# Attention, then a selective scan, on one core: results asked for later, the gate's phase in smaller steps, B and C in the pool of delta u

## The chip, the core and the metric

The kernel runs on one core of one Trainium2 chip. The metric is the device time of one execution in microseconds; the median of several executions counts. Profiles are of one execution each. The engines have short names: PE (TensorE, matmuls; PEld its weight loads), DVE (VectorE), ACT (ScalarE), POOL (GpSimd) and SP (SyncE, which issues the DMAs; SPq is its queue). "L994" is line 994 of the kernel.

## What is computed

There are 16 images of 256 channels by 1024 positions, in f32. Each goes through two layers, and every layer adds to its input what it makes of the group norm of it:

```python
x = x + attention_block(group_norm(x))   # layer norm, 4 heads of 32, softmax, out projection,
                                         # layer norm, feed forward with gelu, residuals
x = x + scan_block(group_norm(x))
# scan_block, L = 1024, 512 inner channels, 64 states:
ctx = sigmoid(conv3(x) + gate_b)
u, z = split(x @ in_proj.T)
u = silu(causal_conv4(u) + conv_b)
dt, B, C = split(u @ x_proj.T)
delta = softplus(dt @ dt_proj.T + dt_b)
h[t] = exp(delta[t] * A) * h[t-1] + (delta[t] * u[t]) * B[t]     # 512 x 64 states, over t
y[t] = sum over states of h[t] * C[t]
out = ((y + u * D) * silu(z)) @ out_proj.T * ctx
```

## The kernel before

**The scan, in units.** The states of one image are 256 tiles of 128 rows by 1024 positions: two channels times 64 states each. One tile is a *unit*. For a unit, SP loads `delta u` of its two channels, spread over the 64 states, into a tile `dub` of the pool `dutp` (`load`, L972); POOL multiplies it by B (`inputs`, L977); PE forms delta in all rows (`decay`, L986) and ACT its exponential in PSUM (L988); DVE scans along the positions (`scan`, L994). Loads run 6 units ahead, products 4, decays 2. The PSUM pool of the decays has two tiles, so PE can begin the decay for unit n + 2 only when the scan of unit n has ended. Eight units fill one tile `h`, and while the next eight are scanned, `outputs` (L1011) reduces it over the states with small matmuls against C: 16 pieces `(r, s)` of 16 matmul records each, two pieces at each step, then copies and a store. There are two tiles `h`, used in turn, so the scan that begins a tile waits until PE has read its old content. B and C lie spread over 128 rows in the tiles `bt` and `ct` of the pool `hst`, one buffer each, loaded when the first unit of an image is loaded (L958 to L963). `ct` is read early in the image (`spread_c`, L1000), `bt` by every product.

**Beside the scan.** While image b is scanned, the other work runs in between: the norm, attention and scan inputs of image b + 1 (`first_norm`, `attention_layer`, `scan_inputs`), and the gate, output projection and store of image b - 1 (`gate_and_store`). Each is a generator that issues some instructions and then yields a *share*. The loop at the end (L1073 to L1114) issues, for each unit, the load, the product, a step of `outputs`, the scan, the decay and then as many steps of the side work as are due. A share under 1 is waited for as it is; a larger one is divided by a rate, but is at least one unit. `rate_for` chooses the rate so that the side work fills 247 of the image's 256 units; it is fed by the shares that the first `prepare(0)` yielded and by the list `GATE` (L859), which stands for the gate's. At unit 250 what is left is issued at once, and the next image but one is loaded.

**Order.** The instructions of PE, ACT, DVE and POOL are held in the order in which they are issued in the program (L1125 to L1135). So an instruction on DVE that follows a matmul in the same step stands behind the unit's scan, and PE does that matmul behind the unit's decay. `psum` takes a bank from the two of pool `mm`, `psum3` from these and the one of `accp` in turn; outside the scan both take free banks from a larger set.

**The places that the change touches.** `group_norm` (L272): sums over a group by PE in two steps, then the reduction on DVE (`mean_of`, L282); twice, for mean and variance. `first_norm` (L369) takes the first loads of the gate along (`besides`). In `attention_layer`: the difference of the two halves of the keys, `kd` (L448); `evacuate` (L521), which copies a head's values (`ao`) and its softmax sums from PSUM (L523, L524), once right behind the last value matmuls and once a step later; the reciprocal of the sums, which goes through DRAM three times (L567 to L586, `den`, `few`); `ao` times the reciprocal (L591), the out projection (L600) and its addition (L596, L605); the residual add of the image (L615), the feed forward (L618, L625, L635, L631). In `scan_inputs` the step before the first tap of the convolution (L749). In the gate's phase: `gate_loads` (L861), the four steps that form `(y + D u) * z` (L883 on DVE, L887 on POOL), the projection `project` (L905, four matmuls of two records each), `join` with the context (L916), the turn back into channel order (`turn_back`, L918) and its addition to the residual (`finish`, L900).

Of the kernel before, what the change touches and what calls it, by code (L numbers as in the profile page):

```python
# [3 lines left out]

# [15 lines left out]
P = 128  # L20
C = 256
KC = C // P
L = 1024
# [27 lines left out]
def attention_then_scan_kernel(  # L51
# [30 lines left out]
    dutp = pool("dutp", 7)  # L82
# [189 lines left out]
    def group_norm(src, dst):  # L272
# [18 lines left out]
        yield 1  # L291
# [15 lines left out]
        yield 1  # L307
# [61 lines left out]
    def first_norm(b, besides=()):  # L369
# [9 lines left out]
        yield from along(group_norm(xs, gn), fetches(tok, pos) + [None] * 3 + list(besides))  # L379
# [5 lines left out]
    def attention_layer(b):  # L385
# [41 lines left out]
        for i in range(2):  # L427
            for hf in range(2):
# [5 lines left out]
                if i == 1:  # L434
                    nc.scalar.copy(k4[:, hs(hf)], ps)
# [12 lines left out]
        nc.vector.tensor_tensor(kd, k4[:, hs(0)], k4[:, hs(1)], ALU.subtract)  # L448
# [118 lines left out]
        den = dram.tile([2, HEADS, L], F32, name="den", tag="den")  # L567
        nc.sync.dma_start(den[0], sums[::DH, :])
        few = small.tile([P, HEADS * L // P], F32, name="few", tag="few")
        rows = [den[i].rearrange("h (p c) -> (h p) c", c=HEADS * L // P) for i in range(2)]  # L570
        yield 1
        nc.sync.dma_start(few, rows[0])
        yield 1
        tok = []
        for go in fetches(tok, kept):
            go()
            yield 0.5
        yield 0.5
        nc.vector.reciprocal(few, few)
        yield 1  # L580
        nc.sync.dma_start(rows[1], few)
        yield 1
        for h in range(HEADS):
            nc.sync.dma_start(sums[ts(h, DH)], den[1, h : h + 1].partition_broadcast(DH))
            if h % 2 == 1:
                yield 0.5  # L586
        yield 0.5
        yield 0.5
        outs = []
        for hf in range(2):  # L590
            nc.vector.tensor_tensor(ao[:, hs(hf)], ao[:, hs(hf)], sums[:, hs(hf)], ALU.mult)  # L591
            for k in range(KC):
                for i, ps in outs:
                    if i == k:
                        t = tok[k][:, hs(0)]
                        nc.vector.scalar_tensor_tensor(t, ps, col("b_out", k), t, ALU.add, ALU.add)  # L596
            outs.clear()
            for k in range(KC):
                ps = psum("o_ps")
                nc.tensor.matmul(ps, wout_s[:, 0, ts(k, P)], ao[:, hs(hf)], start=True, stop=True)  # L600
                outs.append((k, ps))
            yield 1.3
        for k, ps in outs:
            t = tok[k][:, hs(1)]
            nc.vector.scalar_tensor_tensor(t, ps, col("b_out", k), t, ALU.add, ALU.add)  # L605
        del outs, ps
        yield 1.2
# [19 lines left out]
        outs = []  # L627
        for hf in range(3):
            for k, ps in enumerate(outs):
                t = xs[k][:, hs(hf - 1)]  # L630
                nc.vector.scalar_tensor_tensor(t, ps, col("b_ff2", k), t, ALU.add, ALU.add)  # L631
            outs = []
            for k in range(KC if hf < 2 else 0):
                ps = psum("f2_ps")
                nc.tensor.matmul(ps, wff2_s[:, 0, ts(k, P)], hdn[:, hs(hf)], start=True, stop=True)  # L635
                outs.append(ps)
            yield 1.2
# [3 lines left out]
    def scan_inputs(b):  # L641
# [107 lines left out]
        yield 1  # L749
# [109 lines left out]
    GATE = ([0.6, 0.6, 0.4] * ND)[:-1] + [1.3] * 8 + [1]  # L859

    def gate_loads(b):  # L861
# [11 lines left out]
        st["gate"] = ys, us, zs, gs, xs, wo_s, come[4:]  # L873
        return come[:4]

    def gate_and_store(b):
# [20 lines left out]
        def finish():  # L897
            for o, hf, ps in turned:
# [4 lines left out]
            turned.clear()  # L903

        def project(o, k):  # L905
            ps = psum3("m_ps")
            for d in range(ND):
                nc.tensor.matmul(  # L908
                    ps, wo_s[:, d, ts(k, P)], us[d][:, hs(o)],
                    start=(d == 0), stop=(d == ND - 1),  # L910
                )
            return ps

        def join(o, k, ps):
            v = gated[o, k] = hwork("v")
            nc.vector.scalar_tensor_tensor(v, gs[k][:, hs(o)], 1.0, ps, ALU.add, ALU.mult)  # L916
# [11 lines left out]
        work_on = [("p", 0, 0), ("p", 0, 1), ("p", 1, 0), ("t", 0, 0), ("p", 1, 1), ("t", 0, 1), ("t", 1, 0), ("t", 1, 1)]  # L928
        joined = []
        for what, o, i in work_on:  # L930
            for j in joined:
                join(*j)
            joined.clear()
            finish()
            if what == "p":
                joined.append((o, i, project(o, i)))
            else:
                turn_back(o, i)
            if come:
                come.pop(0)()  # L940
            yield 1.3
        finish()
# [248 lines left out]
```

## Time and profile before

| | us |
|---|---|
| times of three runs | 12563.84, 12565.47, 12583.97 |
| median | 12565.47 |
| the profiled execution | 12592.85 |
| its span, first to last instruction | 12590.8 |
| first scan starts | 413.69 |
| first scans of images 6 and 7 (from 0) | 4991.59, 5757.93 |
| granted clock of PE, mean | 0.82 |

The costliest groups of instructions: the columns are line, engine, operation, tiles out and in, count, busy us and mean ns of one, then the idle time of the engine before them and what ended most of it.

```profile
L977 POOL TENSOR_TENSOR dub<-dub,bt 128x1024 f32<-128x1024 f32 x4096 | 9752.7, 2404 | 2130.0 <-DMA dub<-dus 1928.2
L994 DVE TENSOR_TENSOR_SCAN h<-a,dub 128x1024 f32<-128x1024 f32 x4096 | 9166.7, 2273 | 596.0 <-ACT a L988 314.3
L988 ACT ACTIVATE a<-a,acol 128x1024 f32<-128x1024 f32 x4096 | 4466.1, 1090 | 3125.6 <-PE a L986 3065.8
```

The scan and the product for it take most of DVE and POOL. An idle time of an engine costs only where that engine is what the rest waits for.

### The profile page before, as it was taken

The page shows a single profiled execution, that of the slowest core. Times are in us where ns is not written, and L with a number is a line of the kernel's source. Part 1 is how long each engine was busy: PE and PEld are TensorE (multiplying, and loading weights), DVE is VectorE, ACT ScalarE, POOL GpSimd, SP SyncE. Part 2 cuts the span into 40 slices and gives each one's busy share as a digit, 9 for nine tenths or more (in the row PEclk, how much of TensorE's full clock was granted, in tenths as well). Part 3 has the DMA queues.
Part 4 walks back from the last instruction along what each step waited for, and adds up shares of the span by engine and source line. Part 5 has one row for each costly group of instructions (what it writes and reads, how often), then busy time and mean ns, then how long its engine had stood idle before and what let it go on. Part 6 is the DMA issues. An engine that isn't in the chain of part 4 may idle for free.

```text
span 12590.8 us, 419601 instructions
## 1 busy us (share of the span) xinstructions
PE 9574.8 (76%) x183984; PEld 5140.4 (41%) x183984; DVE 11064.3 (88%) x7355; ACT 7506.0 (60%) x10792; POOL 10050.9 (80%) x4233
## 2 busy tenths in 40 slices
PE   6686877868778687886868778687786877868777
PEld 2343434434344343443434344343443434434344
DVE  2788998989989899898989989899898998989998
ACT  3565665656656565665656656566565655656554
POOL 0587878878788787887878878787887878878798
PEclk8887988879788797987879888797887978879756
DMA  1566666676766766666676666766666666676666
GB/s 53 189 229 238 224 221 234 228 243 215 232 235 226 240 225 228 232 226 234 227 238 219 225 233 225 243 218 226 231 227 236 219 225 236 224 239 225 229 238 225
DMA packets 1070400, 2819.80 MB, mean 224 GB/s; under 512 B 324433, under 2 KB 402513, under 8 KB 1068562
## 3 DMA queue, kind: packets, MB, share of 16 engines
q1 hardware_dynamic: 1068562, 2792.97, 65.3%
q8 instruction: 1437, 23.54, 0.8%
q14 instruction: 401, 3.28, 0.1%
HBM read 2513.82 MB, written 261.62 MB: 220 GB/s over the span
## 4 chain that ended last, share of the span: by engine, by line
DVE 37%; PE 31%; issue 13%; ACT 8%; DMA 7%; POOL 3%; SPq 1%; DVEq 0%; POOLq 0%; ACTq 0%
DVE h L994 28%; PE a L986 5%; PE yb L1019 5%; ACT a L988 4%; DMA dub<-dus 3%; POOL dub L977 3%; PE av L535 2%; DVE over L453 2%; PE st_ps L547 2%; PE m_ps L908 2%; PE z_ps L684 2%; PE s_ps L473 2%; DMA xs<-ud 2%; DVE u L720 1%; PE gn_v_ps L275 1%
## 5 line engine op out<-in xcount | busy, mean ns | idle before, releaser
L977 POOL TENSOR_TENSOR dub<-dub,bt 128x1024 f32<-128x1024 f32 x4096 | 9752.7, 2404 | 2130.0 <-DMA dub<-dus 1928.2
L994 DVE TENSOR_TENSOR_SCAN h<-a,dub 128x1024 f32<-128x1024 f32 x4096 | 9166.7, 2273 | 596.0 <-ACT a L988 314.3
L988 ACT ACTIVATE a<-a,acol 128x1024 f32<-128x1024 f32 x4096 | 4466.1, 1090 | 3125.6 <-PE a L986 3065.8
L986 PE MATMUL a<-pieces,pick 48*128 48x512 bf16 x8192 | 1875.8, 448 | 2444.5 <-DVE h L994 2333.4
L1019 PEld LDWEIGHTS yb<-h,cd 128*32 128x32 f32 x131072 | 2433.3, 126 | 2822.9 <-issue 1601.6
L1019 PE MATMUL yb<-h,cd 128*32 128x64 f32 x131072 | 3189.4, 248 | 341.0 <-ACT y L1025 203.3
L986 PEld LDWEIGHTS <-pick 48*128 48x128 bf16 x8192 | 594.4, 95 | 2852.7 <-issue 2194.0
L1025 ACT COPY y<-yb 128x256 f32<-128x256 f32 x2048 | 766.5, 374 | 699.1 <-PE yb L1019 691.4
L1031 PE MATMUL yb<-turn,y 128*32 128x16 f32 x32768 | 590.7, 214 | 5.3 <-issue 4.4
L555 ACT ACTIVATE pt<-st_ps 128x512 f32<-128x512 f32 x1024 | 554.3, 599 | 63.8 <-PE st_ps L547 62.6
L535 PE MATMUL av<-pt,vv 128*64 128x512 f32 x2048 | 588.9, 655 | 3.8 <-ACT sums L524 1.6
L547 PE MATMUL st_ps<-sp 33*128 33x512 f32 x2048 | 573.6, 626 | 3.3 <-ACT pt L555 3.3
L1031 PEld LDWEIGHTS yb<-turn,y 128*32 128x32 f32 x32768 | 572.4, 159 | 6.0 <-issue 4.5
L1035 ACT COPY yo<-yb 128x128 f32<-128x128 f32 x512 | 136.4, 266 | 488.9 <-PE yb L1031 472.3
L734 PE MATMUL g_ps<-xp,w 128*128 128x512 f32 x732 | 406.9, 668 | 0.0
L473 PE MATMUL s_ps<-kd,qm 64*128 64x512 f32 x1022 | 340.6, 612 | 21.2 <-DVE kd L448 14.6
L453 DVE CUSTOM_DVE_ANT_0 over<-s_ps,over 128x512 f32<-128x512 f32 x512 | 325.9, 671 | 24.7 <-PE s_ps L473 24.4
L720 DVE SCALAR_TENSOR_TENSOR u<-up,cwh,u 128x1024 f32<-128x1024 f32 x192 | 295.8, 1541 | 28.0 <-ACT u L712 27.7
L481 ACT ACTIVATE over<-s_ps 128x512 f32<-128x512 f32 x511 | 275.2, 594 | 41.4 <-PE s_ps L473 41.4
L908 PE MATMUL m_ps<-xs,w 128*128 128x512 f32 x504 | 279.2, 704 | 10.2 <-POOL xs L887 9.4
L706 PE MATMUL u_ps<-xp,w 128*128 128x512 f32 x512 | 280.0, 674 | 1.5 <-ACT u L712 1.4
L661 POOL TENSOR_TENSOR xp<-xp,xs 128x1024 f32<-128x1024 f32 x32 | 75.1, 2349 | 254.1 <-DVE xp L313 246.5
(183 smaller groups left out, 7316.7 us busy)
## 6 DMA issues: line engine op xcount, KB each, us to landing
dub<-dus SPq DMA_DIRECT2D x4096, 512.0 KB
dps<-pc SPq DMA_DIRECT2D x384, 128.0 KB
pieces<-dps SPq DMA_DIRECT2D x1024, 48.0 KB
xs<-in_x_dram SPq DMA_DIRECT2D x64, 512.0 KB
xs<-kept SPq DMA_DIRECT2D x64, 512.0 KB
zs<-z SPq DMA_DIRECT2D x64, 512.0 KB
ud<-u SPq DMA_DIRECT2D x64, 512.0 KB
dus<-du SPq DMA_DIRECT2D x64, 512.0 KB
```

The costliest lines, as they stand in the source:

```text
L453: nc.vector.tensor_tensor_reduce(r, s, r, 1.0, -3.0e38, ALU.add, ALU.max, mx[:, at : at + 1])
L473: nc.tensor.matmul(s, qm[c // NJ][r, c % NJ], keys[r], start=True, stop=True)
L535: nc.tensor.matmul(av[ts(e, 2 * DH)], vv[j // (NJ // 2)][:, j % (NJ // 2), 2 * pair + e, :], pts[e], start=(j == 0), stop=(j == NJ - 1),)
L547: nc.tensor.matmul(s, ka[r, ts(j, P)], qa[r, hs(hf)], start=True, stop=True)
L555: nc.scalar.activation(pt, s, AF.Exp)
L977: nc.gpsimd.tensor_tensor(v, v, blocks[units[n][0]]["bt"], ALU.mult)
L986: nc.tensor.matmul(a[:, hs(hf)], w, pieces[r], start=True, stop=True)
L988: nc.scalar.activation(a, a, AF.Exp, scale=acol[:, at : at + 1])
L994: nc.vector.tensor_tensor_scan(now["h", e][:, i, :], decays.pop(n), loaded.pop(n), 0.0, ALU.mult, ALU.add)
L1019: nc.tensor.matmul(yb[ts(g, 32), ts(s, 64)], cd[:, at // 16, ts(c, 32)], hbuf[:, :, at : at + 8], start=(c == 0), stop=(c == 1),)
L1025: nc.scalar.copy(y2[:, r], yb[:, :256])
L1031: nc.tensor.matmul(some[ts(r, 32), x], y2[:, r, x:256:8], turn[:, x], start=True, stop=True)
```

## The change

- `group_norm`: the share behind the second pair of sums is 2, not 1, so the reduction comes later; likewise behind the second projection before the first tap.
- `first_norm`: six loads of the gate go along with the norm in place of four, and begin one step earlier.
- Keys: `kd` reads the second half of the keys from PSUM; a step of its own follows.
- Softmax sums: the copy out of PSUM is DVE's, not ACT's. The reciprocal no longer goes through DRAM: small matmuls bring the sums onto 128 rows, DVE takes the reciprocal from PSUM, ACT spreads it, PE turns it back, and `ao` is multiplied by it out of PSUM. The out projection and the second feed forward matmul share one routine with one bank per step; the residual add L615 is POOL's.
- Gate: the projections are issued in halves by a written plan with 15 steps in place of 8, each result used a step or more later; `GATE` grows accordingly.
- `outputs`: the last step but one takes three pieces, the last one.
- `bt` and `ct` are taken from `dutp`, which has 9 tiles, not 7.
- In the last image the side work begins at unit 12, not 8.

```diff
-    dutp = pool("dutp", 7)
+    dutp = pool("dutp", 9)
...
         sum_of(src[1], s, 1)
-        yield 1
+        yield 2
...
         del qs, q
-        yield 1
+        yield 2
...
-        yield from along(group_norm(xs, gn), fetches(tok, pos) + [None] * 3 + list(besides))
+        yield from along(group_norm(xs, gn), fetches(tok, pos) + [None] * (2 if besides else 8) + list(besides))
...
                     nc.scalar.copy(k4[:, hs(hf)], ps)
+                    keys = ps
...
-        nc.vector.tensor_tensor(kd, k4[:, hs(0)], k4[:, hs(1)], ALU.subtract)
+        nc.vector.tensor_tensor(kd, k4[:, hs(0)], keys, ALU.subtract)
+        yield 1
...
-            nc.scalar.copy(sums[ts(h, DH), hs(hf)], av[o + DH : o + 2 * DH])
+            nc.vector.tensor_copy(sums[ts(h, DH), hs(hf)], av[o + DH : o + 2 * DH])
...
-        den = dram.tile([2, HEADS, L], F32, name="den", tag="den")
-        nc.sync.dma_start(den[0], sums[::DH, :])
...
-            nc.sync.dma_start(sums[ts(h, DH)], den[1, h : h + 1].partition_broadcast(DH))
...
+        for j in range(NJ):
+            nc.tensor.matmul(ps[:, j], sums[:, ts(j, P)], ident[:, ::DH], start=True, stop=True)
+        fetch(tok, kept, 0)
+        yield 2
+        nc.vector.reciprocal(few, ps)
+        wide_few = work("wide_few").rearrange("p (j h d) -> p j h d", j=NJ, h=HEADS)
+        nc.scalar.copy(wide_few, few.unsqueeze(3).to_broadcast([P, NJ, HEADS, DH]))
+        wide_few = wide_few.rearrange("p j h d -> p j (h d)")
+        fetch(tok, kept, 1)
+        yield 2
+        inv = []
+        for hf in range(2):
+            ps = psum3("inv_ps")
+            for j in range(NJ // 2):
+                w = wide_few[:, hf * (NJ // 2) + j]
+                nc.tensor.matmul(ps[:, ts(j, P)], w, ident, start=True, stop=True)
+            inv.append(ps)
+            yield 1
+
+        def times(hf):
+            nc.vector.tensor_tensor(ao[:, hs(hf)], ao[:, hs(hf)], inv[hf], ALU.mult)
...
+        def outputs_of(w, x, to, bias, ahead=None):
+            a, c = output(w, x, 0, 0), output(w, x, 0, 1)
+            if ahead:
+                ahead()
+            yield 1.4
+            add_to(to, a, bias, 0, 0)
+            add_to(to, c, bias, 0, 1)
+            a = output(w, x, 1, 0)
+            yield 1
+            add_to(to, a, bias, 1, 0)
+            c = output(w, x, 1, 1)
+            yield 1
+            add_to(to, c, bias, 1, 1)
+            yield 1
...
+        yield from outputs_of(wout_s, ao, tok, "b_out", partial(times, 1))
...
-            nc.vector.tensor_tensor(xs[hf], xs[hf], tok[hf], ALU.add)
-            ps = psum("f1_ps")
+            nc.gpsimd.tensor_tensor(xs[hf], xs[hf], tok[hf], ALU.add)
+            ps = psum3("f1_ps")
...
+        yield from outputs_of(wff2_s, hdn, xs, "b_ff2")
...
         project(0, 1)
-        yield 1
+        yield 2
...
-    GATE = ([0.6, 0.6, 0.4] * ND)[:-1] + [1.3] * 8 + [1]
+    GATE = ([0.6, 0.6, 0.4] * ND)[:-1] + [1.3] * 9 + [1] * 6
...
-        st["gate"] = ys, us, zs, gs, xs, wo_s, come[4:]
-        return come[:4]
+        st["gate"] = ys, us, zs, gs, xs, wo_s, come[6:]
+        return come[:6]
...
+        def project(o, k, part):
+            if part == 0:
+                banks[o, k] = psum3("m_ps")
+            for d in (2 * part, 2 * part + 1):
                 nc.tensor.matmul(
-                    ps, wo_s[:, d, ts(k, P)], us[d][:, hs(o)],
+                    banks[o, k], wo_s[:, d, ts(k, P)], us[d][:, hs(o)],
                     start=(d == 0), stop=(d == ND - 1),
                 )
...
-        work_on = [("p", 0, 0), ("p", 0, 1), ("p", 1, 0), ("t", 0, 0), ("p", 1, 1), ("t", 0, 1), ("t", 1, 0), ("t", 1, 1)]
...
+        plan = "p000 p001 p010 p011j00 p100 p101j01 t00 p110j10 p111f t01 j11 t10f t11 f f"
+        for what in plan.split():
...
-            yield 1.3
-        finish()
+            yield 1.3 if "p" in what else 1
...
-            bt = hst.tile([P, L], F32, name="bt", tag="bt")
-            ct = hst.tile([P, L], F32, name="ct", tag="ct")
+            bt = dutp.tile([P, L], F32, name="bt", tag="dub")
+            ct = dutp.tile([P, L], F32, name="ct", tag="dub")
...
-                if s % 2 == 1:
+                if s % 2 == 1 and (r, s) != (3, 1) or (r, s) == (3, 2):
                     yield
...
-        if at >= (1 if b + 1 < B else 8):
+        if at >= (1 if b + 1 < B else 12):
```

More of the change, by code (lines that the diff above doesn't have):

```diff
@@ L3 @@
 from itertools import chain, cycle
+from re import findall
 import concourse.bass as bass
@@ L564, in attention_layer @@
             yield 1
-        den = dram.tile([2, HEADS, L], F32, name="den", tag="den")
-        nc.sync.dma_start(den[0], sums[::DH, :])
-        few = small.tile([P, HEADS * L // P], F32, name="few", tag="few")
-        rows = [den[i].rearrange("h (p c) -> (h p) c", c=HEADS * L // P) for i in range(2)]
-        yield 1
-        nc.sync.dma_start(few, rows[0])
-        yield 1
[L574 to L583, printed above, removed]
-            nc.sync.dma_start(sums[ts(h, DH)], den[1, h : h + 1].partition_broadcast(DH))
[L585 to L601, printed above, removed]
-            yield 1.3
@@ L603, in attention_layer @@
[L603 to L607, printed above, removed]
+        tok = []
+        few = small.tile([P, NJ, HEADS], F32, name="few", tag="few")
+        ps = psum("few_ps")[:, : NJ * HEADS].rearrange("p (j h) -> p j h", h=HEADS)
+        for j in range(NJ):
+            nc.tensor.matmul(ps[:, j], sums[:, ts(j, P)], ident[:, ::DH], start=True, stop=True)
+        fetch(tok, kept, 0)
@@ new lines, in times, with output, add_to @@
+        def times(hf):
+            nc.vector.tensor_tensor(ao[:, hs(hf)], ao[:, hs(hf)], inv[hf], ALU.mult)
+        def output(w, x, hf, k):
+            ps = psum3("o_ps")
+            nc.tensor.matmul(ps, w[:, 0, ts(k, P)], x[:, hs(hf)], start=True, stop=True)
+            return ps
+        def add_to(to, ps, bias, hf, k):
+            t = to[k][:, hs(hf)]
+            nc.vector.scalar_tensor_tensor(t, ps, col(bias, k), t, ALU.add, ALU.add)
+        def outputs_of(w, x, to, bias, ahead=None):
[12 more added lines that the diff above has]
+            yield 1
@@ L609, in attention_layer @@
+        times(0)
+        yield 1
+        yield from outputs_of(wout_s, ao, tok, "b_out", partial(times, 1))
+        del inv, ps, wide_few
         xs = []
@@ L626, in attention_layer @@
         yield 2
[L627 to L637, printed above, removed]
+        del f1, ps
+        yield from outputs_of(wff2_s, hdn, xs, "b_ff2")
         state[b]["xs"] = xs
@@ L748, in scan_inputs @@
         project(0, 1)
-        yield 1
+        yield 2
         for d in range(ND):
@@ L897, in finish @@
         def finish():
-            for o, hf, ps in turned:
+            for o, hf, ps in turned[:1]:
                 t = xs[o][:, hs(hf)]
@@ L902, in finish, with join @@
                     nc.sync.dma_start(out[b, ts(o, P), :], xs[o])
[L903 to L907, printed above, removed]
+            del turned[:1]
+        banks = {}
+        def project(o, k, part):
+            if part == 0:
+                banks[o, k] = psum3("m_ps")
+            for d in (2 * part, 2 * part + 1):
                 nc.tensor.matmul(
-                    ps, wo_s[:, d, ts(k, P)], us[d][:, hs(o)],
+                    banks[o, k], wo_s[:, d, ts(k, P)], us[d][:, hs(o)],
                     start=(d == 0), stop=(d == ND - 1),
                 )
-            return ps
-        def join(o, k, ps):
+        def join(o, k):
             v = gated[o, k] = hwork("v")
-            nc.vector.scalar_tensor_tensor(v, gs[k][:, hs(o)], 1.0, ps, ALU.add, ALU.mult)
+            nc.vector.scalar_tensor_tensor(
+                v, gs[k][:, hs(o)], 1.0, banks.pop((o, k)), ALU.add, ALU.mult
+            )
         def turn_back(o, hf):
@@ L926, in turn_back @@
             turned.append((o, hf, ps))
-        work_on = [("p", 0, 0), ("p", 0, 1), ("p", 1, 0), ("t", 0, 0), ("p", 1, 1), ("t", 0, 1), ("t", 1, 0), ("t", 1, 1)]
[L929 to L933, printed above, removed]
-            finish()
[L935 to L938, printed above, removed]
+        plan = "p000 p001 p010 p011j00 p100 p101j01 t00 p110j10 p111f t01 j11 t10f t11 f f"
+        for what in plan.split():
+            for go in findall("p...|j..|t..|f", what):
+                args = [int(c) for c in go[1:]]
+                if go[0] == "p":
+                    project(*args)
+                elif go[0] == "j":
+                    join(*args)
+                elif go[0] == "t":
+                    turn_back(*args)
+                else:
+                    finish()
             if come:
                 come.pop(0)()
-            yield 1.3
-        finish()
+            yield 1.3 if "p" in what else 1
         yield 1
```

## The prediction

> **What bounds the kernel now.** I read the busy table first: it asks which engine could fill the span alone.
>
> ```profile
> span 12590.8 us, 419601 instructions
> PE 9574.8 (76%) x183984; PEld 5140.4 (41%) x183984; DVE 11064.3 (88%) x7355; ACT 7506.0 (60%) x10792; POOL 10050.9 (80%) x4233
> ```
>
> DVE leads, but a share of the span hides stages. So I took one batch of 256 scans in the middle (from the first scan at 4991.6 us to the next batch's at 5757.9, 766.3 us; it carries the gate of the batch before it and the preparation of the one after it) and asked for what DVE waited for in it.
>
> ```profile
> DVE h L994 <- ACT a L988: 20.5, 22, 2.7
> DVE v L916 <- PE m_ps L908: 9.9, 4, 5.0
> DVE h L994 <- PE yb L1019: 7.7, 7, 3.6
> DVE gn_s L282 <- PE gn_v_ps L275: 7.2, 2, 3.7
> DVE h L994 <- POOL dub L977: 7.1, 3, 6.1
> DVE gn_s L282 <- PE gn_m_ps L275: 4.6, 2, 3.8
> DVE xs L883 <- DMA xs<-ud: 4.1, 1, 4.1
> DVE xs L883 <- issue: 2.4, 1, 2.4
> DVE kd L448 <- ACT k L435: 1.6, 1, 1.6
> ```
>
> The columns are total us, number of waits and longest. With the smaller rows DVE's waits add up to about 70 us of the 766; the rest is DVE's own work. So a batch is that work plus those waits, and what the change is worth is read from the two. The work between two scans is a "unit"; a scan starts every 2.2 us if nothing else is on DVE. Then I cut the batch into stages, to see where another engine stands behind the waits.
>
> ```profile
> 5037.30:5060.00 22.70, 9.23 (x242) 6.38 (x235) 16.05 (x10) 7.03 (x10) 19.51 (x8) 0.50 0.93 357
> 5060.00:5098.50 38.50, 35.47 (x445) 21.25 (x448) 27.43 (x20) 11.57 (x16) 27.21 (x12) 0.89 0.71 234
> 5247.30:5381.90 134.60, 123.77 (x2506) 58.96 (x2505) 118.40 (x53) 106.50 (x164) 121.62 (x53) 0.95 0.69 231
> 5496.30:5528.00 31.70, 30.63 (x474) 14.66 (x474) 29.30 (x22) 19.12 (x27) 27.18 (x12) 0.91 0.71 235
> ```
>
> After the length come PE, PEld, DVE, ACT, POOL busy, PE's granted clock, the DMA share, GB/s. The gate's loads (row 1) fill the DMA engines to 0.93; its projections (row 2) fill PE, as do the attention scores (row 3) and z (row 4). There a wait of DVE is PE's backlog, and asking later for the result only moves it.
>
> **Part by part, per batch.** *B and C from the pool.* SP's queue at the batch's end:
>
> ```profile
> 5737.38 1.06 SPq L362 DMA_DIRECT2D xs<-in_x_dram  x2
> 5748.84 0.52 SPq L962 DMA_DIRECT2D bt<-rows  x1
> ```
>
> and POOL at the same time:
>
> ```profile
> 5744.14 4.67 POOL L977 TENSOR_TENSOR dub<-dub,bt 128x1024 f32<-128x1024 f32 x2
> 5755.52 30.03 POOL L977 TENSOR_TENSOR dub<-dub,bt 128x1024 f32<-128x1024 f32 x13 [6.70 <-DMA dub<-dus]
> ```
>
> The single buffer of B is read until POOL's last product, 5744.14 + 4.67 = 5748.81; only then does SP issue B's load, with the next delta u loads queued behind it. SP stands still for 10.4 us, POOL for 6.7, the first scan for 6.1. With nine slots, six loaded tiles and the old B leave two for the new B and C, so SP goes on at 5738.4. One load fewer in flight for some units costs 2.2 us of POOL's lead. Gain 6.0 (bounds 3 and 6.1), at 15 boundaries: 90 us.
>
> *Reductions of the norms one step later.* Waits 7.2 + 4.6 = 11.8. But PE's timeline shows the first pair of sums queued in one unit:
>
> ```profile
> 4996.78 5.45 PE L275 MATMUL gn_m_ps<-xs,share 128*128 128x512 f32 x8
> 5002.15 0.65 PE L1019 MATMUL yb<-h,cd 128*32 128x64 f32 x32
> 5002.74 0.39 PE L986 MATMUL a<-pieces,pick 48*128 48x512 bf16 x2
> ```
>
> The decay that the scan after next needs stands behind them and ends at 5003.1, its exponential (1.09) at 5004.3; a scan moved ahead of the reduction (end 5002.26 + 0.69) finds nothing to follow it until then. Of this wait 3.8 I count 0.4, of the other wide ones 2.5 each, of the short one 0.6, less 0.9 because the second norm's scaling then comes one unit, not two, behind its logarithm. Gain 5.1 (bounds 2 and 11.8).
>
> *The gate.* Waits 9.9 + 1.0 (L900) and 4.1 + 2.4. The plan goes from 9 to 16 steps, so PE's eight pieces (four projections of 3.63, four turns of 2.06 in the timeline, 22.8) lie over 15 units, each with 0.39 of decay and 0.65 of output: 38.4, plus some 3 at half clock at the start. DVE has 15 x 2.22 + 8 x 0.69 = 38.8. So about 43 us against 36.6 (9 units before) + 6 x 2.27 = 50.2: 7.5 gained, not 10.9. The loads two tiles further ahead: a tile of u is asked for two units (8 us with their side work) before use in place of one; of 6.5 I count 5, as the DMA engines are nearly full. Gain 12.5 (bounds 5 and 17.4), in 14 batches: 175 us. On SP these loads stand before delta u loads; POOL's lead, 15 us there, covers that.
> Here "TensorE: Matmul & The Clock Gate" (section on the HAM clock gate) speaks against the change: it says the clock halves after an idle window of about 3.4 us. The rows agree that it halves (0.50, then 0.89); if spreading left it at 0.5, the 22.8 would be 45.6 and the gate would lose 15 instead of gaining 7.5. At 38.4 of 43 PE is hardly idle, so I take the 0.89.
>
> *Keys.* The difference reads PSUM, not a second SBUF tile. L448 takes 1.88 here (1.0 in the median), L354 with one PSUM operand 0.67. "VectorE: DVE Perf Modes" (section on the TRN2 errata) gives PSUM sources a larger fixed term (120 cycles against 58), so by the page the three such edits (kd, twice L591) would cost 0.06 more each; by the rows, beside a busy POOL, they save 0.5 each. The row decides. With the wait: 1.6 + 0.5 = 2.1.
>
> *Softmax sums, outputs.* DRAM round trips go (waits 0.8 + 0.5), L591 saves 1.0, the residual add (L615, mean 1.53, two) goes to POOL: 3.1. POOL pays 4.7; it is at 630 of 766, its lead covers it. Added: eight small matmuls and eight of a turn, 32 records, about 8 us of PE (by the gate's turn, 2.06 for eight records), an ACT copy of about 1.05; I charge 1.0 (bounds 0 and 4) for the decays behind. Gain 4.4.
>
> *One earlier piece of the scan's outputs*: of 0.65 for two pieces one moves, seven waits (7.7): at most 2.3; 1.5.
>
> *Sums copied on DVE.* Eight copies, 32x512 from PSUM. No such row on DVE; between the memset of that length (0.485) and L354 (0.67), which also reads PSUM: I take 0.66, 5.3. Four stand right behind their own matmuls in the same step. Queued behind each is the next scan, so all wait. Price from PE's timeline at such a step:
>
> ```profile
> 5278.00 0.39 PE L986 MATMUL a<-pieces,pick 48*128 48x512 bf16 x2 [0.37 <-DVE h L994]
> 5278.32 1.08 PE L535 MATMUL av<-pt,vv 128*64 128x512 f32 x4
> ```
>
> The scan ended just before 5278.00, the values end at 5279.40: 1.5 us, times four 6.0. ACT loses 8 x 0.577 = 4.6 (L524), and DVE waits for ACT in this stage, so 3 come back. Cost 8.3 (bounds 4 and 20, the latter at half clock).
>
> *At nothing.* The longer step before the first tap: the planner's arithmetic still puts it one unit on, and its wait (1.5) stays; this costs nothing either. The bank for L618 from three in place of two, the last batch's later start of its gate (POOL bounds that batch: 256 products of 2.404 are 615 us, and it takes 612; if that cover were gone, the few units of delay cost nothing as its gate is spread over the whole batch) and the gate after the last scan, whose end waits for its loads and for PE's same matmuls in the same number: 0, bounds -5 and 5.
>
> *A denser plan.* The shares grow from 272.3 to 285.5 over the same 247 units. The planner's arithmetic packs the scores into 48 units, not 53, and z and the x projection into one or so fewer each. A unit removed takes 2.2 us of scan away, but only 0.39 + 0.65 of PE: in PE-bound stages up to 1.15 of new idling, 7 units, 8 us at most; PE is at 92% in the largest, so half: 4 (bounds 0 and 8).
>
> **Sum.** In each of 15 batches: 5.1 + 2.1 + 4.4 + 1.5 - 8.3 - 4 = 0.8, so 12 us. With 90, 175, and 5 in the prologue (the round trips there take 230.9 to 240.7 on the chain of waits, the new path about half) that is 282. The profiled execution took 12592.85 (span 12590.8), so 12311; it stood 0.22% over the median 12565.47, so on that scale 12284. ACT's 20.5 I leave as they are: they are what is late next.
>
> **Rivals.** *The waits vanish as meant*: 6.0 x 15, 17.4 x 14, and 11.8 + 2.1 + 5.4 + 2.3 - 8.3 = 13.3 x 15, with 5: 538, so about 12030. For it: most waits have one cause each. Against: PE at 92 to 97% in the stages named.
> *The backlog only moves*: gate 6, norms 3, keys 2.1, sums 3.5, outputs 1, against 13: 6.0 x 15 + 6 x 14 - 3.4 x 15 + 5 = 128, about 12440. For it: the worked norm above, and DMA at 0.93.
> *Slower: the copies on DVE in the attention scores*, eight in each batch. The rest gains 282 + 15 x 8.3 = 406; they decide from 27 us a batch, 3.4 a copy, which needs half clock and all eight behind fresh matmuls. At 30 to 33 it ends 40 to 85 us slower, about 12630. Against: four of them find results a unit old, and the clock is 0.95.
>
> **Chances.** Likeliest 0.45 (12180 to 12380), vanish 0.18, moves 0.25, slower 0.12. A measurement tells 0.2%, some 25 us. Faster 0.85, same 0.04, slower 0.11. The range 12100 to 12480 leaves out the slower case and the far end of the first rival.
>
> **What would show it.** Right: the first scan of a batch no longer waits for POOL; L916 waits under 4 us; a wait of about 1.5 us before four of the eight sums copies; L282 waits of 2 us left in the first reduction, more waiting for ACT's exponentials. Wrong: batches not near 747 us, PE's clock at 0.5 through the gate, copies on DVE behind waits of 3 us, or the old B still holding SP.

## The result and the profile after

The kernel after the change takes 12875.74 us (median; 12853.06 to 12887.12) against 12571.45 us of the kernel before beside it. The ratio is 1.0239, 95% interval 1.0221 to 1.0257: about 300 us slower, where 282 us of gain were forecast.

The busy table of the kernel after; PE and ACT do about the same work as before, and DVE is busy for as many microseconds (11093.8, before 11064.3) of a longer span, so the loss is waiting and not work:

```profile
span 12874.1 us, 420602 instructions
PE 9793.8 (76%) x184496; PEld 5274.2 (41%) x184496; DVE 11093.8 (86%) x7451; ACT 7502.8 (58%) x10680; POOL 10151.5 (79%) x4265
```

The image in the middle that was shown of before now runs from 5121.05 to 5908.34, 787.3 us. What DVE waits for in it (total us, times, longest):

```profile
DVE h L1004 <- ACT a L998: 33.4, 30, 2.8
DVE sums L527 <- ACT ao L526: 23.9, 8, 4.5
DVE h L1004 <- PE yb L1029: 14.4, 9, 4.2
...
DVE gn_s L283 <- PE gn_m_ps L276: 1.7, 1, 1.7
...
DVE xs L889 <- DMA xs<-ud: 1.3, 2, 0.7
```

Most waits that the change aimed at are gone or short: the gate's join (9.9) has no row any more, its loads fell from 6.5 to 1.3, the norms' reductions from 11.8 to 1.7, POOL's products from 7.1 to 2.8. But a new row stands second: the eight copies of the softmax sums, now on DVE, wait 23.9 us for *ACT's copy of the values*. And the scans themselves wait more, for ACT's exponentials (20.5 to 33.4) and for PE to have read an old tile `h` (7.7 to 14.4).

Two stages of that image, to lay beside the rows shown of before (columns as there): the gate's projections and the attention scores.

```profile
5188.96:5235.25 46.29, 43.44 (x736) 26.13 (x736) 40.57 (x26) 20.38 (x26) 42.15 (x20) 0.92 0.71 252
5382.27:5539.61 157.34, 126.90 (x2408) 58.67 (x2397) 115.29 (x59) 101.03 (x155) 119.09 (x51) 0.85 0.53 181
```

The second row went wrong: 157.3 us for the scores where before took 134.6 in the window shown, at a granted clock of 0.85 in place of 0.95. To compare stages with different numbers of units I take the length of a stage less 2.2 us for each unit in it, and call the rest its excess (means over images 1 to 14 of the profiled executions, worked out from the starts of the scans; the stages left out add up to 85.9, 86.8 and 86.8):

| excess, us per image | before | after | after, sums copied by ACT (`e1_sums_on_act`, below) |
|---|---|---|---|
| boundary of images, first norm | 15.8 | 13.8 | 13.4 |
| gate: loads and multiply-adds | 13.7 | 10.5 | 10.7 |
| gate: projections | 15.9 | 11.1 | 10.9 |
| attention scores (53, 49, 49 units) | 15.9 | 49.4 | 16.0 |
| softmax | 7.1 | 6.9 | 5.2 |
| second norm, then z | 9.9 + 8.1 | 9.8 + 9.5 | 10.4 + 9.5 |
| convolution | 27.0 | 26.4 | 26.4 |
| last ten units | 6.2 | 1.0 | 0.9 |
| a whole image, length | 768.7 | 788.4 | 753.4 |

### The profile page after: what moved, and what is told of

It is laid out like the page before. It is cut to its first block, busy times and chain, and to the rows that moved or that the text cites. A ratio compares the mean times of both kernels' runs of the same rounds, so it can differ in the third digit from the quotient of the medians.

```text
span 12874.1 us, 420602 instructions
## 1 busy us (share of the span) xinstructions
PE 9793.8 (76%) x184496; PEld 5274.2 (41%) x184496; DVE 11093.8 (86%) x7451; ACT 7502.8 (58%) x10680; POOL 10151.5 (79%) x4265
## 4 chain that ended last, share of the span: by engine, by line
DVE 37%; PE 37%; issue 12%; ACT 8%; DMA 4%; POOL 1%; SPq 0%; DVEq 0%; POOLq 0%; ACTq 0%
DVE h L1004 27%; PE yb L1029 6%; PE a L996 6%; ACT a L998 4%; PE st_ps L550 3%; PE av L538 3%; DMA dub<-dus 3%; DVE over L456 2%; PE z_ps L690 2%; PE m_ps L917 2%; PE s_ps L476 2%; PE yb L1041 2%; POOL dub L987 1%; DVE u L726 1%; PE qk_ps L432 1%
## 5 line engine op out<-in xcount | busy, mean ns | idle before, releaser
L550 PE MATMUL st_ps<-sp 33*128 33x512 f32 x2048 | 623.8, 689 | 3.3 <-ACT pt L558 3.3
L527 DVE COPY sums<-av 32x512 f32<-32x512 f32 x128 | 88.2, 689 | 456.0 <-ACT ao L526 431.3
L726 DVE SCALAR_TENSOR_TENSOR u<-up,cwh,u 128x1024 f32<-128x1024 f32 x192 | 274.9, 1432 | 33.5 <-ACT u L718 33.3
L690 PE MATMUL z_ps<-xp,w 128*128 128x512 f32 x508 | 277.5, 673 | 1.4 <-ACT z_t L696 1.4
```

Of the source, the lines that this page charges most:

```text
L550: nc.tensor.matmul(s, ka[r, ts(j, P)], qa[r, hs(hf)], start=True, stop=True)
```

## The experiments

### The suspect: who copies the sums

`e1_sums_on_act` is the kernel after with that one copy back on ACT.

```diff
-            nc.vector.tensor_copy(sums[ts(h, DH), hs(hf)], av[o + DH : o + 2 * DH])
+            nc.scalar.copy(sums[ts(h, DH), hs(hf)], av[o + DH : o + 2 * DH])
```

> The changed kernel with the copy of the softmax sums given back to ACT; all else as changed. Theory A (the copy on DVE waits for ACT's copy of the values out of the same PSUM bank, which stands behind exponentials in ACT's queue; this is the loss): the score stage, 157 us for 49 units, falls to some 125 to 130, the batch from 788 to about 760, the whole from 12876 to about 12430, 1% under the kernel before. Theory B (the denser plan loads PE in the score stage, wherever the copy is): only the copies' own 0.69 us times 8 come back, 83 us in all, so about 12790.

Measured: 12383.16 us, ratio to before 0.9842 (0.9823 to 0.9861). The rest of the change is faster than before; this line alone costs 12875.74 - 12383.16 = 493 us, 32.8 per image. That is theory A, with 47 us more gained than its number (12430); theory B (12790) falls. In the same image the scores took

```profile
5191.24:5315.29 124.05, 114.14 (x2310) 53.06 (x2299) 109.76 (x50) 101.06 (x158) 113.77 (x49) 0.99 0.67 223
```

with the clock at 0.99. `e2_before_sums_dve` makes the same edit the other way in the kernel before:

```diff
-            nc.scalar.copy(sums[ts(h, DH), hs(hf)], av[o + DH : o + 2 * DH])
+            nc.vector.tensor_copy(sums[ts(h, DH), hs(hf)], av[o + DH : o + 2 * DH])
```

> The kernel before with this one edit: the copy of the softmax sums on DVE. Theory A: each of the 128 copies waits about 3 us for ACT and takes 0.69, so DVE loses some 3.5 us eight times a batch in 15 batches, about 430 us: near 13000. Theory B: the copies' own time, about 80 us: near 12655.

Measured: 13022.0 us, ratio 1.034 (1.0325 to 1.0356), 434 us over before, as theory A had it. The line costs nearly as much with nothing else changed, so it needs neither the denser plan nor the new reciprocal. The group's row in the profile, of after and then of this kernel (count, busy us and mean ns of one, then DVE's idle time before it and what ended it):

```profile
L527 DVE COPY sums<-av 32x512 f32<-32x512 f32 x128 | 88.2, 689 | 456.0 <-ACT ao L526 431.3
```

```profile
L524 DVE COPY sums<-av 32x512 f32<-32x512 f32 x128 | 88.2, 689 | 430.7 <-ACT ao L523 393.0
```

A copy is 0.69 us, as priced (0.66); the wait before it is 3.4 us (431.3 in 127), and in images 1 to 14 the eight wait 23.6 us. How it comes about is seen in one step of after, on three engines. DVE:

```profile
5404.31 4.47 DVE L1004 TENSOR_TENSOR_SCAN h<-a,dub 128x1024 f32<-128x1024 f32 x2 [0.72 <-ACT a L998]
5412.23 0.68 DVE L527 COPY sums<-av 32x512 f32<-32x512 f32 x1 [3.46 <-ACT ao L526]
5412.95 2.29 DVE L1004 TENSOR_TENSOR_SCAN h<-a,dub 128x1024 f32<-128x1024 f32 x1
5419.42 0.69 DVE L527 COPY sums<-av 32x512 f32<-32x512 f32 x1 [4.18 <-ACT ao L526]
```

ACT:

```profile
5411.62 0.58 ACT L526 COPY ao<-av 32x512 f32<-32x512 f32 x1
5415.94 1.09 ACT L998 ACTIVATE a<-a,acol 128x1024 f32<-128x1024 f32 x1 [3.74 <-PE a L996]
5417.70 1.09 ACT L558 ACTIVATE pt<-st_ps 128x512 f32<-128x512 f32 x2 [0.67 <-PE st_ps L550]
5418.81 0.58 ACT L526 COPY ao<-av 32x512 f32<-32x512 f32 x1
```

PE:

```profile
5407.60 1.02 PE L550 MATMUL st_ps<-sp 33*128 33x512 f32 x4
...
5410.47 1.08 PE L538 MATMUL av<-pt,vv 128*64 128x512 f32 x4
...
5415.29 0.61 PE L996 MATMUL a<-pieces,pick 48*128 48x512 bf16 x2 [3.16 <-DVE h L1004]
5415.69 1.92 PE L550 MATMUL st_ps<-sp 33*128 33x512 f32 x4
```

The values stand in PSUM from 5411.55 (5410.47 + 1.08). ACT copies its half, and DVE's copy begins only at its end, 5412.2, although the two copies read different partitions: the trace shows DVE's instruction waiting for ACT's semaphore at these places. Of the first wait of 3.46 us, 2.8 are for the values and the rest is for ACT's copy. At the second copy this is the whole wait. Its values have been there since 5411.55, but ACT's copy stands in ACT's queue behind an exponential of the scores, which needs PE's scores; PE's scores stand behind the decay; the decay waits 3.16 us for the scan; and the scan stood behind the first copy. After those 3.16 us PE needs 0.61 for the decay, not 0.39, and 1.92 for four score matmuls, not 1.02: it runs at half clock. So the second wait is longer than the first.

The half clock outlasts these two waits. It sets in at 5414.83, after 2.7 us in which PE stood idle, and holds for 20.5 us, though PE is busy for 15.6 of them:

```profile
5414.83:5435.31 20.48, 15.59 (x172) 6.56 (x172) 12.22 (x7) 8.95 (x13) 11.73 (x6) 0.50 0.37 134
```

What is said on this by the Trainium skill, "PSUM — Partial Sum Buffer" (section on bank collisions), points the other way and the run decides: the page wants two engines kept apart within one bank *and* 32-partition quadrant, reads too, while different quadrants of one bank can be read at once. The two halves of `av` are two quadrants, so by that no order is needed; here the two are ordered nevertheless, and the order is that of issue, as the next run shows. What puts the order into the program stays open.

### Splitting the price: order and distance

`e3_dve_first` is the kernel after with the two copies issued in the other order, so that ACT waits for DVE and not DVE for ACT.

```diff
-            nc.scalar.copy(ao[ts(h, DH), hs(hf)], av[o : o + DH])
             nc.vector.tensor_copy(sums[ts(h, DH), hs(hf)], av[o + DH : o + 2 * DH])
+            nc.scalar.copy(ao[ts(h, DH), hs(hf)], av[o : o + DH])
```

> The changed kernel with the two copies of a head issued in the other order: DVE's copy of the sums first, ACT's of the values second. Theory A: DVE no longer stands behind ACT's queue, only, four times a batch, behind PE's value matmuls (1.5 us): 24 us of waits a batch become about 6 to 8, the whole about 12610 to 12640. A second theory, that DVE waits for PE and PE's half clock and ACT is only the last name on the chain: waits stay above 15 us a batch, the whole above 12750.

Measured: 12626.07 us, ratio 1.0034 (1.0021 to 1.0048), as theory A had it. The order alone is worth 12875.74 - 12626.07 = 250 us, 16.6 per image. In the scores of this kernel, first DVE's waits before the copies, then the stage:

```profile
DVE sums L526 <- PE av L538: 8.2, 4, 2.9
```

```profile
5293.62:5433.52 139.90, 123.29 (x2320) 56.70 (x2312) 115.33 (x58) 98.87 (x153) 117.07 (x51) 0.90 0.57 199
```

This is the case that the prediction had costed: four copies wait for their own matmuls, the other four not at all. The waits are 8.2 (6.0 predicted), and still the kernel is 12626.07 - 12383.16 = 243 us, 16.2 per image, above ACT's copies: 8.2 + 8 x 0.69 = 13.7, and the other 2.5 go with a clock that fell from 0.99 to 0.90.

`e9_late_copy` is the kernel after with DVE's copies kept in a list and issued at the beginning of the next step of the side work, when both the values and ACT's copy are old.

```diff
-            nc.vector.tensor_copy(sums[ts(h, DH), hs(hf)], av[o + DH : o + 2 * DH])
+            late.append((sums[ts(h, DH), hs(hf)], av[o + DH : o + 2 * DH]))
...
                 for j in range(NJ):
+                    copy_late()
```

> The changed kernel, the sums still copied by DVE behind ACT's copy from the same bank, but each copy held back to the next side step, when ACT's copy is a unit or more old. Theory A: the waits (24 us a batch) and with them the half clock and its later waits go; what stays is the copying itself, 8 x 0.69 a batch, 83 us over 12383: about 12470. Rival: DVE reading that bank while PE and ACT work in the others is what costs, wherever it stands: above 12550.

Measured: 12485.89 us, ratio 0.9922 (0.9903 to 0.9941), near theory A's 12470; the rival (above 12550) falls. With the waits all but gone (1.9 per image are left) the stage is back at clock 0.97,

```profile
5259.58:5386.80 127.22, 114.59 (x2338) 53.81 (x2330) 114.64 (x57) 98.70 (x153) 115.20 (x50) 0.97 0.65 219
```

and what remains against ACT's copies is 12485.89 - 12383.16 = 103 us, 6.8 per image; the eight copies' own time is 5.5 of it. So of the 32.8 per image, about 6.8 are DVE's own work and what is left of waits, some 9 the copies' closeness to their matmuls, and 16.6 the order behind ACT.

### Is it the denser plan?

`e4_before_denser` is the kernel before with its planner's rate raised to what the change makes it, and nothing else.

```diff
+            rate *= 1.097 if b + 1 < B else 1.0
```

> The kernel before with the planner's rate multiplied by 1.097, which packs the side work as the change does (scores into 48 to 49 units) and leaves units without side work at the end. Theory A: 0 to 4 us a batch, so 12570 to 12635. Theory B: 15 us a batch or more, above 12800.

Measured: 12800.59 us, ratio 1.0163 (1.0147 to 1.0179). The number lies at the edge of theory B's (above 12800), but not for the reason that was to be tried: the scores lost only 3.0 us per image and z 1.2, as the prediction had it for the PE-bound stages (4), so the denser plan does not explain the 33.5 that the scores lose in the change. But the kernel before has no later results to fill the denser plan, so everything with a fixed latency gets closer to its user: the second norm's scaling, for one. In the kernel before, and then here, what its DVE instruction L313 waited for (us, times):

```profile
  ACT gn_v_ps L310: 3.2, 1
```

```profile
  ACT gn_v_ps L310: 46.8, 15
```

One wait of 3.1 us in each of 14 images that was not there, 4.4 in that stage, and 5.0 in the softmax, where the round trips through DRAM are. A density is not an edit that can be tried by itself: this kernel shows what a denser plan costs where no later results fill it.

### What the other parts are worth

Each of these takes one part back from `e1_sums_on_act` (12383.16). The intervals of these ratios leave some 40 us open in each difference, 3 per image, so their sizes are rough. Figures by stage are of the profiled executions; that of `e1_sums_on_act` lies 16 us under its median.

`e5_gate_back`: the gate's phase as before (the list `GATE`, four loads along, whole projections in 8 steps).

```diff
-    GATE = ([0.6, 0.6, 0.4] * ND)[:-1] + [1.3] * 9 + [1] * 6
+    GATE = ([0.6, 0.6, 0.4] * ND)[:-1] + [1.3] * 8 + [1]
...
-        plan = "p000 p001 p010 p011j00 p100 p101j01 t00 p110j10 p111f t01 j11 t10f t11 f f"
+        work_on = [("p", 0, 0), ("p", 0, 1), ("p", 1, 0), ("t", 0, 0), ("p", 1, 1), ("t", 0, 1), ("t", 1, 0), ("t", 1, 1)]
```

> The changed kernel with the sums' copy on ACT (12383 us), and the gate's phase as it was: plan, loads, list of shares. Theory A (an edit is worth what its own stage shows): the gate's two stages lost 8.0 us of excess a batch in 14 batches, so 112 come back: about 12495. Theory C (a result asked for later is paid back by the denser plan that its shares force on the other stages): with 6 shares fewer the other stages get some 4 us a batch back, so only about 55 us: near 12440. The prediction's own term, 12.5 a batch: 12560.

Measured: 12461.74 us, ratio 0.9897 (0.9865 to 0.9929); the gate's part is worth 79 us, where 175 were predicted, between theory A (112) and theory C (55). By stages it gains 9.5 per image in the gate itself and gives 1.5 back in the layer norm and 3.7 in the convolution.

`e6_pool_back`: B and C in buffers of their own, `dutp` with 7 tiles.

```diff
-    dutp = pool("dutp", 9)
+    dutp = pool("dutp", 7)
...
-            bt = dutp.tile([P, L], F32, name="bt", tag="dub")
+            bt = hst.tile([P, L], F32, name="bt", tag="bt")
```

> The changed kernel with the sums' copy on ACT (12383 us), and B and C in their own single buffers again, seven tiles for delta u. The prediction's term, 6.0 at 15 boundaries: about 12473. Rival: the wait only hides POOL's lag behind the scans of the last ten units and part of it stays with the new pool: half, about 12430. No shares change, so theories A and C agree.

Measured: 12456.83 us, ratio 0.9899 (0.987 to 0.9927): 74 us for the pool, 90 predicted, and half of it by the rival; 5.0 per image in the last ten units.

`e7_norms_back`: the reductions of the norms one step earlier again.

```diff
-        yield 2
+        yield 1
         m = s[:, :NG]
...
-        yield 2
+        yield 1
         v = s[:, :NG]
```

> The changed kernel with the sums' copy on ACT (12383 us), and the reductions of the norms one share earlier again. The prediction's term, 5.1 in 15 batches: about 12460. Theory C: waits of 11 us for PE come back at the reductions, but waits of the scans for exponentials go and the plan is 4 shares less dense: 12350 to 12410, no difference that can be told or a gain.

Measured: 12319.23 us, ratio 0.9789 (0.9762 to 0.9816), the best of all and 267 us better than before. The norms' later results *cost* 64 us in this company, where 77 us of gain were predicted. Not all of it is theirs: the two profiled executions differ by 54 us, of which 11 lie before the first scan, 11 in the first image and 29, 2.1 per image, in images 1 to 14. `e8_reciprocal_back`: the reciprocal through DRAM.

```diff
+        den = dram.tile([2, HEADS, L], F32, name="den", tag="den")
+        nc.sync.dma_start(den[0], sums[::DH, :])
...
-            nc.tensor.matmul(ps[:, j], sums[:, ts(j, P)], ident[:, ::DH], start=True, stop=True)
```

> The changed kernel with the sums' copy on ACT (12383 us), and the reciprocal through DRAM again, with ao times it from a second SBUF tile; the output routine and the residual add on POOL stay as changed. The prediction's term (waits 1.3, products 1.0, less 1.0 for PE) 1.3 a batch and 5 in the prologue: about 12408. Theory C (in the denser plan the round trips come too late, as in the run of the kernel before with the denser plan, where this stage lost 5.0 us a batch): 12450 to 12470.

Measured: 12440.94 us, ratio 0.9884 (0.9857 to 0.991): 58 us for the matmul way, between the prediction's term (25) and theory C (67 or more); 3.9 per image in the softmax stage and 1.9 in the scores.

### Why later norms cost

The same image's waits of DVE, in `e1_sums_on_act` and in `e7_norms_back`:

```profile
DVE gn_s L283 <- PE gn_m_ps L276: 2.1, 1, 2.1
DVE xp L314 <- ACT gn_v_ps L311: 2.0, 1, 2.0
DVE xs L602 <- PE o_ps L597: 2.0, 2, 1.0
DVE u L726 <- ACT u L718: 1.9, 1, 1.9
```

```profile
DVE gn_s L283 <- PE gn_v_ps L276: 6.5, 2, 3.8
DVE gn_s L283 <- PE gn_m_ps L276: 6.3, 2, 4.0
```

The later reductions take 10.7 us of waiting away there, and bring 2 us of waiting at each of three other places: the second norm's scaling, the feed forward's addition, the first tap of the convolution. Over images 1 to 14 the reductions' waits fall by 11.2 per image and these, z's and the scans' rise by 9.6, while DVE's own work grows by 2.8: the waits about cancel, and the loss is in the work. Of the 2.8, 2.5 are longer multiply-adds of the gate (1.3) and of the convolution (1.3); why they are longer is seen at the end of this section. Two reasons stood: the longer plan packs all else more tightly (theory C), or what matters is at which unit each step lands. `e10_norms_back_denser` raises the rate of `e7_norms_back` to what the later norms had made it:

```diff
+            rate *= 1.02 if b + 1 < B else 1.0
```

> The kernel with the sums' copy on ACT and the norms' reductions early (12319 us), with the planner's rate multiplied by 1.02, so that its plan is as dense as with the later reductions (rate 1.298 in place of 1.273). Theory C (density alone undoes the later reductions): 12370 to 12390. Rival (it is where the later reductions stand, the second norm's scaling close behind its logarithm, and chance in the prologue, where the two differ by 11 us): 12310 to 12340.

Measured: 12325.8 us, ratio 0.9798 (0.9781 to 0.9814), within 7 us of `e7_norms_back`. Density as such, at this step of 2%, falls; where steps land is what is left.

`e11_fewer_shares` goes the other way, `e7_norms_back` without the keys' own step and with the step before the first tap at 1 again.

```diff
         nc.vector.tensor_tensor(kd, k4[:, hs(0)], keys, ALU.subtract)
-        yield 1
...
         project(0, 1)
-        yield 2
+        yield 1
```

> The kernel with the sums' copy on ACT and the norms' reductions early (12319 us), without the added step behind the keys and with one share, not two, before the first tap: two shares fewer. Theory C: 1 to 2 us a batch faster, 12290 to 12305. Rival (each late result is worth its wait: 1.6 for the keys): 12340 to 12360.

Measured: 12435.65 us, ratio 0.9887 (0.9872 to 0.9902), 116 us slower; both numbers missed by far. So one more kernel, `e12_first_tap_back`, with the second half of that edit alone:

```diff
         project(0, 1)
-        yield 2
+        yield 1
```

> The version with the sums copied by ACT and the norms' reductions as before (12319), with one of the two later results of the run that took both back (12436): only the step before the first tap of the convolution is 1 again, the keys' own step stays. In the run with both taken back, the multiply-adds of the convolution took 4.1 us more per image and waited 1.5 us more (5.6 us per image in the convolution, 84 us in 15 images), and the scores 3.1 us more. Theory A, the step before the first tap carries the loss: about 12400 (12385 to 12425), with the first multiply-add waiting about 1.5 us for ACT again. Rival B, the keys' step carries it: 12345 at most, and the convolution's multiply-adds as short as with both steps (1.38 us in the mean).

Measured: 12495.83 us, ratio 0.9937 (0.9921 to 0.9954). That one number costs 177 us beside `e7_norms_back`, more than with the keys' step gone as well. Theory A has the place right: the convolution loses 6.7 us per image (5.6 expected). B falls. The size is missed again: the scores lose 3.5 more, the first image 19 us, the time before the first scan 10, and the stages between the rest. Part of the convolution's loss is a wait for ACT before the first multiply-add, 1.9 per image. The larger part is no wait at all. The multiply-adds' durations (minimum, median, maximum in ns) in `e7_norms_back` and in `e12_first_tap_back`:

```profile
L769 DVE SCALAR_TENSOR_TENSOR u<-up,u x64: 1224/1316/2499, 306.3 to 11509.8; 128x1024 f32<-128x1024 f32 x64
```

```profile
L769 DVE SCALAR_TENSOR_TENSOR u<-up,u x64: 1192/1832/3360, 317.4 to 11696.7; 128x1024 f32<-128x1024 f32 x64
```

The same instruction takes 1.2 to 3.4 us, depending on when it is issued; with L726 the multiply-adds take 4.7 us more per image in `e12_first_tap_back`. "SBUF — State Buffer" (sections "SBUF: two separate sides" and "Who interferes with whom") gives a reason: a DVE instruction with two SBUF inputs and a GpSimd instruction that reads SBUF exclude each other, and the later one waits for the whole of the other. The trace of `e12_first_tap_back` agrees, in the longest of these multiply-adds and in the next of that line:

```profile
4803.61 3.36 DVE L769 SCALAR_TENSOR_TENSOR u<-up,u 128x1024 f32<-128x1024 f32 x1
4803.54 2.35 POOL L987 TENSOR_TENSOR dub<-dub,bt 128x1024 f32<-128x1024 f32 x1 [1.09 <-DMA dub<-dus]
4826.60 1.20 DVE L769 SCALAR_TENSOR_TENSOR u<-up,u 128x1024 f32<-128x1024 f32 x1
```

POOL's product began 0.07 us before the first one and ended at 4805.89; the multiply-add ended 1.08 us later, at 4806.97. POOL stood idle when the second began. So it is with all of them: of the 256 multiply-adds of the convolution (L726 and L769) in this trace, 230 begin while POOL is at work, and each ends 1.08 to 1.19 us after that POOL instruction; the other 26 take 1.19 to 1.29 us. What a multiply-add costs is thus set by how much of POOL's product is left when it comes, and that shifts with the steps around it.

## Why the prediction was wrong, by its own steps

**Sums copied on DVE, the step that failed.** The text took 8.3 us per image (bounds 4 and 20), and 32.8 were measured. It has three terms. The copies themselves, 5.3, are 5.5. "The scan ended just before 5278.00, the values end at 5279.40: 1.5 us, times four": four copies do wait for their matmuls, 8.2 in `e3_dve_first`; but in the change all eight wait, 23.6 in the mean image, because the next link was not looked for. The text named what is queued *behind* the copy (the scan), and not what the copy itself waits for besides its matmul: ACT's copy from the same bank, and all that stands ahead of it in ACT's queue. "ACT loses 4.6, so 3 come back": no sign of it is seen; even in `e3_dve_first` the cost is 2.5 above waits and work, not 3 below.

The text's third rival had the place, the half clock and the price, 30 to 33 us per image (40 to 85 us slower; by its own sum 44 to 89). But it put all eight "behind fresh matmuls", and four of them stood behind ACT's queue alone: that its price fits is in part luck. Its argument against, "four of them find results a unit old", was true of PE's results and beside the point. Its point of decision was off too: it set 27 us per image against a rest of 406 us. The rest was 204 (12587.53 - 12383.16), so already from 13.6 per image, 1.7 a copy, the change is slower; already `e3_dve_first` is.

**The clock gate.** The halving of the clock was weighed against the gate's projections, which run at 0.92 as taken. It bites in the scores, where the copies' waits let PE stand idle for 2.9 to 4.5 us at a time, seven times in the image shown: 0.99 to 0.85. Idle stretches have to be looked for at each place where the change makes an engine wait, not only where it moves PE's work.

**The gate: 12.5 predicted, 8.0 in its stages (table), 5.3 in sum** (79 us in 15). The spread is as worked out: 46.3 us for 16 units, PE busy for 43.4, where the text has 43 for 15 units and a unit more of 2.2. The loads gave 3.2 of 5. What was missing is that the steps around it give back 5.2 once they land elsewhere.

**Norms: 5.1 predicted; minus 2.1 in images 1 to 14** (minus 4.3 with all of the 64 us). The reductions' wait goes as said. The text looked for what is late next only right behind the sums (decay, exponential), and charged one place, the second norm's scaling, 0.9; that scaling, the feed forward and the first tap wait 2 us each. The second rival, "the backlog only moves", is right on the waits of this part; the longer multiply-adds are in no rival.

**B and C: 6.0 predicted, 4.9** (74 us in 15). B's load now leaves SP at once when the image changes, and POOL's lead is what the first scan sees. SP in after:

```profile
5889.22 1.25 SPq L363 DMA_DIRECT2D xs<-in_x_dram  x2
5890.84 0.52 SPq L972 DMA_DIRECT2D bt<-rows  x1
5893.02 0.52 SPq L972 DMA_DIRECT2D ct<-rows  x1
```

The 10.4 us of standing still are 0.4 before B and 1.7 before C.

**Softmax and outputs: 4.4 predicted, about 3.9** for the reciprocal (58 us in 15; the move of the addition to POOL was not tried alone). **Keys: 2.1 predicted.** The difference takes 0.69 in place of 1.16 and waits 16.3 us in all in place of 32.5: 1.5 per image. Here the price per edit was right, and the trace gives the reason: with two SBUF inputs the difference took 0.67 to 2.17 us in before, and with one of them in PSUM it takes 0.66 to 0.69 in after, POOL busy or not. But its added step alone costs 60 us between `e11_fewer_shares` and `e12_first_tap_back`. **First tap, at nothing:** in the change as it stands its wait stays (1.9), as said; beside the earlier norms the same edit is worth 177 us, as the step then lands two units on. **Outputs, 1.5 predicted:** not tried alone; scans waited for PE's reading of `h` for 120.8 us over the run before and for 177.5 with ACT's copies, so no gain is seen. **Denser plan:** 4 predicted for the stages at PE's limit, 4.2 in `e4_before_denser`; what it does to waits of fixed latency was left out. **Prologue:** a gain of 5 was predicted. It took 413.7 before and 413.1 after, and from 401 to 437 over the experiments, 402 and 422 in two that are the same up to the first scan, so 5 can't be read there.

**Where the expected gain of the rest went.** Without the copies 406 us were expected, 204 came. Waits of DVE over the whole run, before and then in `e1_sums_on_act`:

```profile
DVE h L994 <- ACT a L988: 314.3, 359, 7.5
DVE v L916 <- PE m_ps L908: 139.7, 58, 5.2
...
DVE xs L883 <- DMA xs<-ud: 105.4, 31, 9.0
DVE gn_s L282 <- PE gn_v_ps L275: 97.2, 31, 5.4
DVE gn_s L282 <- PE gn_m_ps L275: 93.7, 33, 6.5
```

```profile
DVE h L1004 <- ACT a L998: 492.2, 513, 3.3
DVE h L1004 <- PE yb L1029: 177.5, 137, 2.9
...
DVE xs L889 <- DMA xs<-ud: 42.1, 29, 8.9
...
DVE gn_s L283 <- PE gn_m_ps L276: 36.8, 15, 8.5
```

The gate's join still waits 11.8 and the variance's reduction 5.5 (rows further down), so these waits fell by 127.9 + 63.3 + 91.7 + 56.9 = 340 us. The scans' waits for their exponentials rose by 178 and for the outputs by 57: a wait of DVE had also been time in which PE and ACT caught up, and when it is gone the scan meets them later in the same stage. That is my reading; part of the rise has another cause, as the denser plan alone (`e4_before_denser`) raised the waits for exponentials by 57 and those for outputs not at all. The text said "ACT's 20.5 I leave as they are: they are what is late next". That names the place, and prices its growth at nothing; with the outputs it took back 235 of these 340.

What stays open: single steps of the plan are worth 60 to 180 us by where they land. How a multiply-add is stretched is seen (beside `e7_norms_back`, 4.7 of the 11.1 us per image that `e12_first_tap_back` loses in images 1 to 14), but the rest is waits in many places, no way was found to tell beforehand which placing is good, and the parts do not add up (79 + 74 + 58 - 64 and the tap's 177 are more than the 204 in all).

## What to carry to other kernels

Before a PSUM read is moved to another engine, ask what else reads that bank: the built program may make the second reader wait for the first, and then the moved instruction inherits the other engine's whole queue. Issue the copy on the engine that everything waits for first, or a step later, or leave it where it was; here the three are 250, 390 and 493 us better. Where a DVE instruction reads two SBUF tiles beside a busy POOL, look at the spread of its durations and not at the median alone. And do not count a removed wait in full until it is clear that the engines which caught up in it don't need it: here about half came.

## What the hardware showed beyond expectation

Waits of DVE of 2.2 to 4.5 us, eight in an image, took PE's granted clock in that stage from 0.99 to 0.85. One stretch of half clock set in after 2.7 us of idling and held for 20.5 us, with PE busy for 15.6 of them; four score matmuls took 1.92 us in it, not 1.02.

Multiply-adds on DVE with two SBUF inputs (128x1024 in f32) ended 1.08 to 1.19 us after the POOL instruction that was at work when they began, all 230 of them in `e12_first_tap_back`, and so took up to 3.36 us; with POOL idle at their start they took 1.19 to 1.29. The time of L769 in an image changed by a third (6.0 to 7.9 us) when the step before the first of them was shortened from two shares to one.
